# A convolution, attention and expert kernel on one core: the first image, its spectra and the last mixing stores change queues at the seam between two stages

## The chip, the cores and the metric

One core of one Trainium2 chip runs the whole program. The metric is the device time of one execution in microseconds (us), as the median of several runs. Busy times, spans and waits come from one profiled execution, whose own time stands beside them.

## What is computed

The input `x` has 32 images of 128 channels and 64 by 64 pixels, in float32. Two layers follow each other:

```
# layer 0: group norm, a 2-D transform along both axes, a mix of channels at each
#          frequency, the inverse transform, and the image is added
x_f  = tensor_product(gn(x), k11, k12)            # complex, 64 x 64
w_f  = tensor_product(weight, kd1, kd2) * 64
prod = einsum('bihw,oihw->bohw', x_f, w_f)
x    = x + real(tensor_product(prod, k21, k22))
# layer 1, on tokens (pixels) of 128 channels
t = t + attention(ln(t), Wk, bk, Wv, bv)          # for each image a 128 x 128 softmax, made over its tokens
t = t + experts(ln(t), router_w, expert_w)        # 8 experts, the best 2 weighed
```

The kernel arranges the attention of layer 1 image by image: a Gram matrix of the normed tokens, the key and value matrices on either side of it, a softmax of 128 x 128, and one product for all tokens.

## The kernel before

The kernel has three stages, each with a plan of its own (`Plan`): operations get an engine, an estimated duration, a due time, what they follow, and the buffers that they take and free; the plan plays this through and the instructions are recorded in the order that comes out. Before the third plan a list `first` is recorded without any plan.

**Stage 1** (to about 940 us) norms and transforms every image and writes its spectrum to `xf` in DRAM.

**Stage 2, the mixing** (to about 2544 us) runs over the 64 frequencies `w`. For each it builds the weights' spectrum (`weights`, L626), multiplies (`mix`, L648) and copies the result from PSUM to the tiles `outs[half]`: ACT copies rows `hh = 0` and DVE rows `hh = 1` (`mix_out`, L658, tile `o`). `store` (L667) then writes each half of the outputs with eight DMAs of 128 KB on SP's queue to `pf` in DRAM. Half 0 holds output channels 0 to 63, half 1 the others.

**Stage 3** runs over the images. The spectrum of image `b` is read back from `pf` in eight tiles `r` (e = 0 to 7, 16 output channels each; `load_r`, L836, two DMAs of 256 KB for each tile, one for 64 partitions). Tiles 0 to 3 need half 0 of the stores, tiles 4 to 7 half 1. Then come the inverse along w (`w_inverse_piece`, L900, tile `pw`, copied to `u` by ACT, L907), the inverse along h (`h_inverse_piece`, L919, tile `pz`, added to the image `y` by DVE, L927), the turn into tokens (L1001, L1006), the statistics and the norm (L973 to L1041), the Gram matrix (L1052), the key and value products (`kv1`, `kv2`, L1069 and L1077), the softmax, the product with the tokens (L1125), the router and the experts (L1276). Images overlap: the experts of one run beside the front of the next ones.

At the seam between stages 2 and 3 the program holds, in this order:

- `prepare` (L780 to L802), first in `first`: the mean over the model dimension is taken out of the expert weights (two matmuls `pm`, L785; DVE L786 and L790), of the key and value weights `wkv` (matmul `pmk`, L793; DVE L794 and L798), and the router's column sums `rws` are made (matmul `pms`, L801; DVE L802).
- The tiles r 0 and 1 of image 0 on GpSimd's queue, r 2 and 3 on ACT's, then r 4 to 7, r 0 and 1 of image 1, and the images `y0` and `y1` (one DMA of 2 MB each, L830) on SP's.
- The loads of the small constants `wkv`, `rb_sb`, `prx`, `kvb` on ACT's queue (L755 to L778). They, and the eight memsets of `rank` on GpSimd (L763), lie in memory that the tiles `o` held before, so they wait for the last stores of `pf`.

Where the recorded instructions of an engine stand decides what waits behind what: all four engines and SP work through their own lists in order. Of DMA completions there are eight semaphores that SP and ACT use in turn, and eight for GpSimd's queue; a DMA that takes a semaphore again waits until the DMA before it on that semaphore has landed.

Of the kernel before, what the change touches and what calls it, by code (L numbers as in the profile page):

```python
# [10 lines left out]
F32 = mybir.dt.float32  # L11
# [5 lines left out]
P = 128  # L17
# [3 lines left out]
NE = 8  # L21
# [69 lines left out]
def kernel(  # L91
# [15 lines left out]
    nc = tc.nc  # L107
    B = x.shape[0]
    xv = x.rearrange("b c h w -> b c (h w)")
# [3 lines left out]
    n = HW  # L113
# [39 lines left out]
    om = cp.tile([P, P], F32, name="om")  # L153
# [9 lines left out]
    with ExitStack() as ph1:  # L163
# [9 lines left out]
        made, xs, zs, vs, tile_of = {}, {}, {}, {}, {}  # L173
        on_pe = []

        def add(key, engine, us, at, run, after=(), take=(), free=(), late=0.0):
            after = [made[k] for k in after if k in made]
            if engine == "PE":
                after += on_pe[-1:]
            made[key] = plan.add(engine, us, SLOT * at, run, after, take, free, late)  # L180
            if engine == "PE":
                on_pe.append(made[key])
# [248 lines left out]
        def store(b, g):  # L431
            def run():
                f = tile_of.pop(("f", b, g))

                for k in range(0, 8, 4):
                    nc.sync.dma_start(xf[b, :, 8 * g + k : 8 * g + k + 4, :], f[:, k : k + 4])
            return run
# [52 lines left out]
        def piece(kind, b, g, at):  # L490
            if not 0 <= b < B:
                return
            if kind == "pz":
                add(
                    ("pz", b, g), "PE", 1.0, at, turn_over(b, g), [("nm", b, k) for k in range(4)],
                    ("ps",), ("x",) if g == 3 else (),
                )
                for r in range(2):
                    add(
                        ("zo", b, g, r), "ACT", 1.2, at, turned(b, g, r),  # L500
                        [("pz", b, g)] + [("pv", b - 2, k) for k in range(8)] + ([("zo", b, 0, 0)] if g or r else []),
                        (), ("ps",) if r else (),
                    )
            elif kind == "pv":
                add(
                    ("pv", b, g), "PE", 1.12, at, along_w(b, g),
                    [("zo", b, k, r) for k in range(4) for r in range(2)] + ["wi"], ("ps",),
                )
                add(
                    ("vo", b, g), "ACT", 1.02, at, w_out(b, g),  # L510
                    [("pv", b, g)] + [("pf", b - 2, k) for k in range(8)] + ([("vo", b, 0)] if g else []), (), ("ps",),
                )
            else:
                add(("pf", b, g), "PE", 1.95, at, along_h(b, g), [("vo", b, k) for k in range(8)], ("ps",))
                on_act = g % 4 == 3
                add(("fo", b, g), "ACT" if on_act else "DVE", 1.02 if on_act else 1.22, at, h_out(b, g), [("pf", b, g)], ("f",), ("ps",))
                add(("fs", b, g), "SP", 0.9, at, store(b, g), [("fo", b, g)], (), ("f",), 5.0)
# [7 lines left out]
        for s in range(B + 2):  # L525
            if s == 0:
                norm(2)
            for g in range(4):
                at = s + 0.25 * g
# [27 lines left out]
            if 12 <= s < 16:  # L557
                k = s - 12
# [7 lines left out]
    with ExitStack() as ph2:  # L566
# [11 lines left out]
        made, tile_of = {}, {}  # L578
# [84 lines left out]
        def store(w, half):  # L663

            for c in range(0, n, 8):
                lo = (half * n + c) * n
                nc.sync.dma_start(  # L667
                    pf[w, :, lo : lo + 8 * n], outs[half][w % 2 * n : w % 2 * n + n, c : c + 8].rearrange("m o h -> m (o h)")
                )

# [21 lines left out]
        def mixed(*after):  # L692

            while rest:
                w, half, g, at = rest.pop()
                add(
                    ("mo", w, half, g, 1), "DVE", 1.25, at + 0.1, lambda: mix_out(w, half, g, 1),
                    [("mo", w, half, g, 0), *after], (), ("m",),
                )
                if g:  # L700
                    add(
                        ("st", w, half), "SP", 0.1, at + 0.2, lambda: store(w, half),
                        [("mo", w, half, g, hh) for g in range(2) for hh in range(2)], (), ("o",), 8.0,
                    )

        for w in range(n):
# [9 lines left out]
            for half in range(2):  # L716
                for t in range(4):
                    at = w + 0.5 * half + 0.125 * t
# [25 lines left out]
    eps = ctx.enter_context(tc.tile_pool(name="eps", bufs=3, space=PSUM))  # L744
# [23 lines left out]
    QX = P + 2 * NE  # L768
    prx = [ct.tile([P, QX], F32, name=f"prx{i}") for i in range(2)]
    for t in prx:  # L770
        nc.scalar.dma_start(t[:, P + NE : QX], router_w)
    rws = ct.tile([P, NE], F32, name="rws")
# [7 lines left out]
    def prepare():  # L780

        for half in range(2):
            es = slice(4 * half, 4 * half + 4)
            pe = eps.tile([P, 512], F32, tag="pe", name=f"pm{half}")
            nc.tensor.matmul(pe, om, ew_sb[:, es, :].rearrange("d e c -> d (e c)"), start=True, stop=True)  # L785
            nc.vector.scalar_tensor_tensor(  # L786
                ebb[:, es, :].rearrange("p e c -> p (e c)"), ebb[:, es, :].rearrange("p e c -> p (e c)"),
                1.0 / P, pe, ALU.mult, ALU.subtract,
            )
        nc.vector.tensor_add(ew_sb, ew_sb, ebb)  # L790

        pe = eps.tile([P, 512], F32, tag="pe", name="pmk")
        nc.tensor.matmul(pe[:, 0 : 2 * P], om, wkv.rearrange("d e c -> d (e c)"), start=True, stop=True)  # L793
        nc.vector.scalar_tensor_tensor(  # L794
            kvb.rearrange("p e c -> p (e c)"), kvb.rearrange("p e c -> p (e c)"), 1.0 / P, pe[:, 0 : 2 * P],
            ALU.mult, ALU.subtract,
        )
        nc.vector.tensor_add(wkv, wkv, kvb)  # L798

        pe = eps.tile([P, 512], F32, tag="pe", name="pms")  # L800
        nc.tensor.matmul(pe[:, 0:NE], om, prx[0][:, P + NE : QX], start=True, stop=True)  # L801
        nc.vector.tensor_scalar_mul(rws, pe[:, 0:NE], float(P))  # L802

    plan = Plan({"cv": 1, "pe": 3, "tl": 3, "r": 10, "x": 2, "xg": NG, "xn": 2, "xT": 2, "tm": 2, "so": 2, "gate": 2})
    SLOT = 114.0
# [16 lines left out]
            engine, us, SLOT * at, run, [made[k] for k in names if k[0] >= 0], take, free, late  # L822
        )

    xs, rs, tile_of, first = {}, {}, {}, [prepare]

    def transfers(b):
        def load_x():
            xs[b] = xp.tile([P, HW, HW], F32, tag="x", name=f"y{b}")
            nc.sync.dma_start(xs[b].rearrange("c h w -> c (h w)"), xv[b])  # L830

        def load_r(e, queue=nc.sync):
            def run():
                t = rs[b, e] = rp.tile([P, 16 * n], F32, tag="r", name=f"r{b}_{e}")
                for r in range(2):
                    queue.dma_start(t[r * n : (r + 1) * n], pfv[b, e, r])  # L836
            return run

        if b == 0:

            first.extend(load_r(e, nc.gpsimd if e < 2 else nc.scalar) for e in range(4))

        for e in range(8):
            early = b == 0 and e < 4
            add(
                b, f"r{e}", "SP", 0.2, b - 0.5 + 0.08 * e, (lambda: None) if early else load_r(e), take=("r",),
                late=0.0 if early else 5.0,
            )
        add(b, "x", "SP", 0.1, b + 0.2, load_x, take=("x",), late=12.0)

    def conv(b):
        def w_inverse(e):
# [113 lines left out]
    def front(b):  # L966
# [53 lines left out]
        for g in range(8):  # L1020
            at = s1 + 0.016 * g
# [36 lines left out]
        for g in range(8):  # L1058
            at = s1 + 0.26 + 0.016 * g
# [45 lines left out]

        at = s1 + 0.40
        add(b, "gs", "DVE", 0.3, at, gsum, ["pg7"], (), ("tl",))
        add(b, "pb", "PE", 0.35, at, kv1, ["gs"], ("tl",))
        add(b, "t1", "DVE", 0.3, at, kv1_out, ["pb"])
        add(b, "pb2", "PE", 0.35, at, kv2, ["t1"])  # L1110
        add(b, "sm", "DVE", 0.5, at, soft1, ["pb2"])
# [45 lines left out]
        for j, lo in enumerate(range(0, NT, 3)):  # L1157
            m = min(3, NT - lo)
            at = s1 + 0.45 + 0.016 * j
# [71 lines left out]
        at = s1 + 0.64  # L1231
# [130 lines left out]
    for b in range(B):  # L1362
        transfers(b)
        conv(b)
        front(b)
        experts(b)
    with tc.manual_schedule():
        for run in first:
            run()
        plan.run()  # L1370

# [32 lines left out]
def build(arrays):  # L1404
    import concourse.bacc as bacc

    nc = bacc.Bacc("TRN2", target_bir_lowering=False, num_devices=1)
    args = [
        nc.dram_tensor(k, a.shape, mybir.dt.from_np(a.dtype), kind="ExternalInput").ap() for k, a in arrays.items()
    ]  # L1410
    shape = arrays["in_x_dram"].shape
    args.append(nc.dram_tensor("out_0_dram", shape, F32, kind="ExternalOutput").ap())
    with tile.TileContext(nc) as tc:
        kernel(tc, *args)
    return nc
# [8 lines left out]
```

## Time and profile before

| | |
|---|---|
| median of 3 runs | 6112.17 us (6111.25 to 6116.16) |
| the profiled execution's own time | 6110.47 us |
| its span, first to last instruction | 6108.6 us |
| busy: PE, weight loads | 5903.2 us (97%), 4682.8 us (77%) |
| busy: DVE, ACT, POOL | 4245.8 us (70%), 3762.1 us (62%), 4183.5 us (68%) |
| last matmul of stage 2 starts to end | 2535.01 us to 2544.56 us |
| first inverse along w (L900) starts | 2567.96 us |

PE is TensorE's matmuls, PEld its weight loads, DVE VectorE, ACT ScalarE, POOL GpSimd, SP SyncE; a q behind an engine's name is its sequencer, which issues DMAs. L667 is line 667 of the kernel. The chain of waits is the work that ended last, followed back from the end: at each step what released it. "Issue" is time in which an engine waited for nothing that the profile shows. A float32 matmul shows as two records, so a piece of 16 matmuls is 32 records.

### The profile page before, as it was taken

What the parts mean: (1) busy time and instruction counts of PE and PEld (TensorE: products, weight loads), DVE (VectorE), ACT (ScalarE), POOL (GpSimd) and SP (SyncE); (2) the same over time, 40 slices, a digit from 0 to 9 for tenths busy, and PEclk for the clock granted to TensorE, in tenths of its full rate; (3) what the DMA queues carried; (4) which work ended last, traced back from release to release, by engine and by line L of the source; (5) the groups of instructions that cost most, each with busy time, mean ns of one, the idle gap of its engine ahead of it and who ended that gap; (6) DMA issues with size and microseconds to landing.
All of it is one profiled execution on the core that took longest, in us unless ns stands there. A gap on an engine that the chain in (4) does not pass through costs nothing.

```text
span 6108.6 us, 219213 instructions
## 1 busy us (share of the span) xinstructions
PE 5903.2 (97%) x95372; PEld 4682.8 (77%) x95372; DVE 4245.8 (70%) x7696; ACT 3762.1 (62%) x7057; POOL 4183.5 (68%) x3753
## 2 busy tenths in 40 slices
PE   7999999999999999889999999999999999999998
PEld 7999998999999999776666666666666666666654
DVE  5565545555555555458878787787878878787888
ACT  7666664555555555366676676666767676666653
POOL 2110006666666666338888888888888888888888
PEclk9999999999999999899999999999999999999999
DMA  5767666666666666632223132221322223132100
GB/s 200 234 228 237 234 211 182 173 175 172 170 172 173 172 173 173 164 87 92 77 62 103 58 97 70 82 86 60 99 65 90 77 66 100 58 97 70 65 25 28
DMA packets 557732, 756.74 MB, mean 124 GB/s; under 512 B 58592, under 2 KB 322784, under 8 KB 552672
## 3 DMA queue, kind: packets, MB, share of 16 engines
q1 hardware_dynamic: 555120, 740.33, 40.7%
q8 instruction: 749, 12.27, 0.9%
q10 hardware_dynamic: 1328, 1.32, 0.1%
q14 instruction: 215, 1.76, 0.1%
q0 software_dynamic: 320, 1.05, 0.1%
HBM read 406.93 MB, written 335.54 MB: 122 GB/s over the span
## 4 chain that ended last, share of the span: by engine, by line
PE 78%; DVE 9%; ACT 3%; DMA 2%; issue 2%; POOL 0%; SPq 0%; ACTq 0%; POOLq 0%; DVEq 0%
PE pe L1276 24%; PE m L648 17%; PE g L626 9%; PE pf L418 5%; PE pu L857 4%; PE pp L1125 4%; PE py L879 4%; PE pg L1052 4%; DVE tm L1287 2%; PE pv L396 2%; DMA out_dram<-so 2%; PE px L1263 2%; DVE eq L1200 1%; DVE eq L1199 1%; PE po L1322 1%
## 5 line engine op out<-in xcount | busy, mean ns | idle before, releaser
L1276 PE MATMUL pe<-ew_sb,xT 128*128 128x512 f32 x4096 | 1964.9, 601 | 80.1 <-DVE tm L1287 75.1
L1287 DVE TENSOR_TENSOR tm<-pe,oh 128x512 f32<-128x512 f32 x2028 | 1348.6, 685 | 360.8 <-PE pe L1276 339.6
L1312 POOL TENSOR_TENSOR tm<-tm 128x512 f32<-128x512 f32 x1014 | 1281.0, 1278 | 229.4 <-DVE tm L1287 205.7
L1276 PEld LDWEIGHTS pe<-ew_sb,xT 128*128 128x128 f32 x4096 | 701.1, 191 | 591.6 <-issue 405.1
L637 DVE COPY f<-g 128x1024 f32<-128x1024 f32 x512 | 627.2, 1225 | 661.3 <-PE g L626 661.3
L648 PE MATMUL m<-f,s 128*64 128x64 f32 x32768 | 1069.0, 224 | 4.8 <-POOL s L599 3.4
L648 PEld LDWEIGHTS m<-f,s 128*64 128x64 f32 x32768 | 998.4, 138 | 66.6 <-POOL s L599 3.7
L599 POOL COPY s<-l 128x512 f32<-128x512 f32 x512 | 545.4, 1099 | 594.0 <-issue 514.6
L637 ACT COPY f<-g 128x1024 f32<-128x1024 f32 x512 | 519.3, 1014 | 574.6 <-PE g L626 548.0
L1315 POOL TENSOR_TENSOR tk<-tk,tm 128x256 f32<-128x256 f32 x1014 | 758.7, 748 | 79.5
L867 ACT COPY u<-pu 64x512 f32<-64x512 f32 x960 | 557.5, 581 | 223.7 <-PE pu L857 214.3
L1313 POOL TENSOR_TENSOR tm<-tm 128x512 f32<-128x512 f32 x507 | 651.5, 1285 | 39.8
L626 PE MATMUL g<-c,wst 9*128 9x128 f32 x16384 | 607.4, 284 | 4.5 <-ACT f L637 3.3
L626 PEld LDWEIGHTS g<-c,wst 9*128 9x128 f32 x16384 | 508.9, 187 | 40.7 <-ACT f L637 4.4
L857 PEld LDWEIGHTS pu<-qw,r 128*128 128x128 f32 x3840 | 464.4, 193 | 93.3 <-issue 68.7
L1138 ACT ACTIVATE pp<-pp,m 128x128 f32<-128x128 f32 x1024 | 444.3, 434 | 136.7 <-PE pp L1125 110.8
L349 POOL TENSOR_TENSOR grstd<-gms,mhalf 128x1 f32<-128x1 f32 x32 | 17.7, 555 | 737.2 <-DVE gms L345 737.2
L601 POOL TENSOR_SCALAR s<-l 128x512 f32<-128x512 f32 x256 | 509.5, 1990 | 0.0
L418 PE MATMUL pf<-ph,v 128*128 128x128 f32 x4096 | 491.4, 278 | 5.4 <-ACT z L383 1.1
L857 PE MATMUL pu<-qw,r 128*128 128x128 f32 x3840 | 471.7, 276 | 8.0 <-ACT u L867 8.0
L418 PEld LDWEIGHTS pf<-ph,v 128*128 128x128 f32 x4096 | 467.1, 192 | 15.4 <-ACT z L383 7.2
L973 DVE BATCH_NORM_STATS2 bs<-tk 128x6 f32<-128x128 f32 x2048 | 453.1, 280 | 21.9 <-ACT tk L1006 7.0
(164 smaller groups left out, 8228.3 us busy)
## 6 DMA issues: line engine op xcount, KB each, us to landing
xf<-f SPq DMA_DIRECT2D x512, 256.0 KB, 3.3
l<-xf SPq DMA_DIRECT2D x1024, 128.0 KB, 3.1
pf<-o SPq DMA_DIRECT2D x1024, 128.0 KB, 3.2
r<-pf SPq DMA_DIRECT2D x504, 256.0 KB, 4.7
x<-in_x_dram SPq DMA_DIRECT2D x256, 256.0 KB, 4.5
y<-in_x_dram SPq DMA_DIRECT2D x32, 2048.0 KB, 11.3
out_dram<-so SPq DMA_DIRECT2D x256, 256.0 KB, 3.8
tw<-in_tw_dram SPq DMA_DIRECT2D x6, 384.0 KB, 6.5
```

Of the source, the lines that this page charges most:

```text
L418: nc.tensor.matmul(pl[:, j * P : (j + 1) * P], vs[b][:, 8 * g + j, :], ph.rearrange("h r m -> h (r m)"), start=True, stop=True,)
L599: nc.gpsimd.tensor_copy(dst, src)
L626: nc.tensor.matmul(pg[g // 2][:, g % 2, m * P : (m + 1) * P], wst[rows, 16 * half + 4 * t + m, :], c[rows].rearrange("r h k -> r (h k)"), ...
L637: copy(f.rearrange("i m (g o) -> i m g o", g=2), tile_of["g", w, half, t][k].rearrange("i g (o m) -> i m g o", o=4))
L648: nc.tensor.matmul(ps[hh * n : (hh + 1) * n, q, :], s[:, h].rearrange("i k b -> i (k b)")[:, B * r : B * r + n], f[:, h, r, :], start=(r = ...
L857: nc.tensor.matmul(ps[:, k, :], rs[b, e][:, k * P : (k + 1) * P], qw.rearrange("w r m -> w (r m)"), start=True, stop=True,)
L867: nc.scalar.copy(u[r * n : (r + 1) * n, :, oh * n + 8 * e : oh * n + 8 * e + 8], ps[oh * n : (oh + 1) * n, :, r * n : (r + 1) * n].rearran ...
L1276: nc.tensor.matmul(ps, tile_of["xT", b, i // 4][:, i % 4, :], ew_sb[:, es, :].rearrange("d e c -> d (e c)"), start=True, stop=True,)
L1287: nc.vector.tensor_tensor(tile_of["tm", b, i // 2][:, i % 2, es, :], tile_of.pop(("pe", b, i, half)).rearrange("p (e c) -> p e c", c=P), t ...
L1312: nc.gpsimd.tensor_tensor(tm[:, k, 0:4, :], tm[:, k, 0:4, :], tm[:, k, 4:8, :], ALU.add)
L1313: nc.gpsimd.tensor_tensor(tm[:, :, 0:2, :], tm[:, :, 0:2, :], tm[:, :, 2:4, :], ALU.add)
L1315: nc.gpsimd.tensor_tensor(t[:, lo : lo + 2, :], t[:, lo : lo + 2, :], tm[:, :, m, :], ALU.add)
```

## The change

Three things change at the seam, and nothing else:

- Of the very last eight stores of `pf` (w = 63, half 1), those with c = 8, 24, 40, 56 go to ACT's queue.
- Image 0 (`y0`) is loaded first of all, in eight DMAs of 256 KB on GpSimd's queue; behind it on the same queue come the tiles r 0 to 5 of image 0. SP keeps r 6 and 7. ACT's queue has no r tile any more.
- `prepare` keeps the expert weights and is recorded after these loads. The rest becomes two operations of the plan: `kvp` on PE (both matmuls into one PSUM tile) after `h0`, and `kvq` on DVE (its three instructions); `kv1` waits for `kvq`.

```diff
             for c in range(0, n, 8):
                 lo = (half * n + c) * n
-                nc.sync.dma_start(
+                queue = nc.scalar if w == n - 1 and half and c % 16 else nc.sync
+                queue.dma_start(
                     pf[w, :, lo : lo + 8 * n], outs[half][...]
                 )
...
-        pe = eps.tile([P, 512], F32, tag="pe", name="pmk")
+    def prepare_front():
+        pe = tile_of["kvp"] = eps.tile([P, 512], F32, tag="pe", name="pmk")
         nc.tensor.matmul(pe[:, 0 : 2 * P], om, wkv.rearrange("d e c -> d (e c)"), start=True, stop=True)
+        nc.tensor.matmul(pe[:, 2 * P : 2 * P + NE], om, prx[0][:, P + NE : QX], start=True, stop=True)
+
+    def prepared_front():
+        pe = tile_of.pop("kvp")
         nc.vector.scalar_tensor_tensor(kvb..., 1.0 / P, pe[:, 0 : 2 * P], ALU.mult, ALU.subtract)
+        nc.vector.tensor_scalar_mul(rws, pe[:, 2 * P : 2 * P + NE], float(P))
         nc.vector.tensor_add(wkv, wkv, kvb)
...
-    xs, rs, tile_of, first = {}, {}, {}, [prepare]
+    xs, rs, tile_of, first = {}, {}, {}, []
...
-            nc.sync.dma_start(xs[b].rearrange("c h w -> c (h w)"), xv[b])
+            if b == 0:
+                for k in range(8):
+                    nc.gpsimd.dma_start(xs[b][:, 8 * k : 8 * k + 8], x[b][:, 8 * k : 8 * k + 8])
+            else:
+                nc.sync.dma_start(xs[b].rearrange("c h w -> c (h w)"), xv[b])
...
-            first.extend(load_r(e, nc.gpsimd if e < 2 else nc.scalar) for e in range(4))
+            first.append(load_x)
+            first.extend(load_r(e, nc.gpsimd) for e in range(6))
...
-        add(b, "pb", "PE", 0.35, at, kv1, ["gs"], ("tl",))
+        add(b, "pb", "PE", 0.35, at, kv1, ["gs", (0, "kvq")], ("tl",))
...
+            add(0, "kvp", "PE", 0.5, 0.5, prepare_front, ["h0"], ("pe",))
+            add(0, "kvq", "DVE", 1.2, 0.5, prepared_front, ["kvp"], (), ("pe",))
...
-        for run in first:
+        for run in (*first, prepare):
             run()
```

More of the change, by code (lines that the diff above doesn't have):

```diff
@@ L797, in prepare @@
         )
+        nc.vector.tensor_scalar_mul(rws, pe[:, 2 * P : 2 * P + NE], float(P))
         nc.vector.tensor_add(wkv, wkv, kvb)
-        pe = eps.tile([P, 512], F32, tag="pe", name="pms")
-        nc.tensor.matmul(pe[:, 0:NE], om, prx[0][:, P + NE : QX], start=True, stop=True)
-        nc.vector.tensor_scalar_mul(rws, pe[:, 0:NE], float(P))
     plan = Plan({"cv": 1, "pe": 3, "tl": 3, "r": 10, "x": 2, "xg": NG, "xn": 2, "xT": 2, "tm": 2, "so": 2, "gate": 2})
@@ L839, in transfers @@
         if b == 0:
-            first.extend(load_r(e, nc.gpsimd if e < 2 else nc.scalar) for e in range(4))
+            first.append(load_x)
+            first.extend(load_r(e, nc.gpsimd) for e in range(6))
         for e in range(8):
-            early = b == 0 and e < 4
+            early = b == 0 and e < 6
             add(
@@ L848, in transfers @@
             )
-        add(b, "x", "SP", 0.1, b + 0.2, load_x, take=("x",), late=12.0)
+        add(b, "x", "SP", 0.1, b + 0.2, load_x if b else (lambda: None), take=("x",), late=12.0 if b else 0.0)
     def conv(b):
@@ L1364 @@
         conv(b)
+        if b == 0:
+            add(0, "kvp", "PE", 0.5, 0.5, prepare_front, ["h0"], ("pe",))
+            add(0, "kvq", "DVE", 1.2, 0.5, prepared_front, ["kvp"], (), ("pe",))
         front(b)
```

## The prediction

> **What bounds the kernel now.** The page first: PE is busy 97% of the span, so a change off PE's path pays only where PE stands still. The clock row and the chain then show one such place beside the end of stage 1: the seam. The chain of waits from 2535 us on:
>
> ```profile
> 2535.08 2.04 PE m L648 x64
> ...
> 2541.86 1.83 SPq L667
> 2543.73 5.59 DMA pf<-o
> 2549.48 0.50 ACTq L836
> 2550.02 1.01 ACT o L658
> 2551.06 1.24 DVE o L658
> 2552.31 5.21 DMA pf<-o
> 2557.54 0.45 SPq L667
> 2558.03 3.25 DMA pf<-o
> 2561.49 4.71 DMA wkv<-in_wkT_dram
> 2566.22 4.31 DMA r<-pf
> 2571.24 9.13 PE pw L900 x237
> 2580.37 3.08 issue
> 2583.45 9.90 PE pw L900 x242
> 2593.44 0.60 ACT u L907
> ```
>
> Columns: start, length, what. The last copy of `o` waits on ACT behind an r load, the last eight stores behind that copy, the constants behind the stores, and PE behind the constants. Who stood idle is told by the timeline (in brackets the idle time before, and what ended it):
>
> ```profile
> 2550.02 1.00 ACT L658 COPY o<-m 64x1024 f32<-64x1024 f32 x1 [8.14 <-DMA pf<-o]
> ...
> 2551.06 1.23 DVE L658 COPY o<-m 64x1024 f32<-64x1024 f32 x1 [3.85 <-ACT o L658]
> ...
> 2561.55 0.30 POOL L763 MEMSET rank<- 128x1 f32 x8 [15.20 <-DMA pf<-o]
> ```
>
> The last `m` ends at 2544.56, so this copy is 5.4 us late for no reason of data. By stretches (busy us of PE, PEld, DVE, ACT, POOL with counts; granted clock; DMA share; GB/s):
>
> ```profile
> 2569.00:2577.00 8.00, 6.70 (x148) 6.51 (x146) 0.92 (x3) 2.35 (x4) 0.00 (x0) 0.59 1.00 245
> 2579.00:2588.00 9.00, 5.92 (x134) 5.83 (x132) 0.00 (x0) 2.35 (x4) 0.00 (x0) 0.69 1.00 411
> ```
>
> In the first only r tiles move, at 245 GB/s (one DMA of 256 KB lands each 1.05 us) with the DMA engines full. In the second the images move at 411 GB/s. PE runs at a clock of 0.59 to 0.69 there: while it does, a piece of `pw` takes 1.7 us, at full clock 0.93 us (the spacing of the `u` copies).
>
> The target is the end of the inverse along w, 2593.4 us. What follows (h inverse, turns, statistics, w inverse of image 1) is PE and ACT in a chain until the steady state; the recorded order of every engine is unchanged from there to the end, so a shift of 2593.4 reaches the end whole.
>
> **The change, step by step.**
>
> *The copies.* Without r 2 in front, ACT copies at 2544.6 to 2545.6. DVE now has one `ebb` operation before its copy, not two: 2545.66 + 0.69, then 1.23: done at 2547.6 instead of 2552.29, 4.7 us earlier.
>
> *The stores.* SP needed 2552.31 to 2558.63 for eight issues (0.45 to 0.65 us each, and a wait for a landing); four on each queue is about 2.4 us. But their semaphores must have come free from the half 0 stores, the last of which landed at 2550.84 beside 1 MB of r loads; now 2 MB of image are beside them. I take issue to 2551 and, at 3.5 to 5 us from issue to landing, all landed by 2554.5 (2552.5 if the image is out of the way, 2557 if it is not) instead of 2561.28: 6.8 us earlier.
>
> *The image.* `y0` waits for the last `m` (it lies where stage 2's tiles lay), so GpSimd issues it from about 2545.1: eight at 0.5 to 0.8 us. Loads of the same shape ran at 406 GB/s at the start of stage 1 (8 to 20 us), so 2 MB need 5.2 us alone and 8 with the stores. They run in 2546 to 2554, when little else can. In itself this gains nothing: `y0` landed at 2585.89 and DVE first needed it at 2599.60. What it buys is 2 MB less between r and `y1`.
>
> *The r tiles, now the bound.* Before, r 0 to 3 had landed by 2557.2; now GpSimd's list is `y0`, the first DMA of r 0, the memsets of `rank` (which wait for all last stores), then eleven DMAs of 256 KB. Their issue starts at about 2555.2 (0.52 us each, never the bound); the first takes 5.2 us to land, as the quickest of the four on this queue did (up to 6.1): PE starts `pw` at 2560.4 instead of 2567.96, and without the 3.28 us in which it stood for `kvb`. The eleven DMAs are 2.9 MB. Alone at 250 GB/s r 5 would land at 2570. From 2561 SP brings r 6, 7 and image 1's r 0, 1 beside them (seven DMAs after its first one, each held until a constant on ACT has landed), then `y1`. No row shows two queues of r loads side by side: from 245 GB/s together (r rows) to 342 (r and stores, 2556 to 2558). At 310, half for each, GpSimd needs 1.7 us for 256 KB: with 1.5 us to land, r 2 at 2566, r 3 at 2569.5, r 4 at 2573, r 5 at 2576, or 2580 where the 16 KB packets of `y1` come beside its last ones; I take 2578. Bounds for r 5: 2570 and 2584.
>
> *PE.* Tiles 0 to 3 at about 3.4 us each in the slow clock follow the data, tile 4 to 2576.5, tile 5 to 2581, tiles 6 and 7 another 3.7 us (full clock) to 6.8: `pw` ends at 2585, bounds 2580 (data early, clock up at half-way) and 2591, instead of 2593.4: **8.4 us earlier**.
>
> *Key and value preparation.* Its two matmuls (1.19 and 0.43 us) and three DVE operations (0.42, 0.16, 0.42) leave the start and go between the fourth and fifth of the eight `pz` pieces, each 0.69 us of DVE to 0.93 or 1.7 of PE. PE's 32 free records at the slow clock cover part of the DVE time; a `pz` piece three places on waits for the shared PSUM buffers. I charge **1.2 us** (0.6 to 2). `kv1` comes over 40 us later (2652): the added wait costs nothing.
>
> *Instruction gaps.* The "issue" gaps of 3.08 and 3.52 us (2594.64) in PE come while the instruction queue's 16 KB packets arrive among full DMA engines. The engines stay full, so I leave them in; either can go or a third come: 3.5 us each way.
>
> Sum: 8.4 - 1.2 = 7.2 us less than the profiled execution's 6110.47 (span 6108.6 and 1.9 around it): 6103.3. The median stands 1.7 us above that execution, so **6105.0 us**.
>
> **A rule against the change.** The row: at 2556 to 2558 stores on SP's queue and r loads on ACT's moved together at 342 GB/s. The Trainium skill, "DMA: Bandwidth & Descriptors", section "Issuing engines are not separate DMA queues", says that queues of different engines run on the same 16 DMA engines and that spreading saves only the time of issuing. By it the split of the stores would be worth the 3 us of issue, and two r streams would share 245 GB/s: 2.1 us for each of the last eight DMAs instead of 1.7, 3.2 us later, 6108 on the median's scale. The trace's 342 is for another mix, so it does not refute it.
>
> **Rivals.**
>
> *More comes free (0.31).* Two streams, mostly to different halves of the partitions, run near the 342; r 5 lands at 2572 and PE, busy from 2560, gets the full clock by 2574: `pw` ends at 2580 (13.4 earlier), and with `y0` gone one instruction gap goes too (up to 3.5). For it: `y0` and `y1` held the DMA engines full through 2579 to 2593. Against: SP's r 6, 7 and the next image's compete with tiles that are needed first. 13.4 + 1.5 - 1.2 = 13.7: 6098.5.
>
> *Given back (0.20).* r 0 to 5 behind `y0` on one queue arrive so late that the early start is only a longer wait: r 5 at 2583 to 2584, `pw` at 2590 to 2592: 0 to 2 us less, 6110 to 6112. In this case the change doesn't do what it says.
>
> *Slower (0.10).* GpSimd's queue starves beside SP's, which has `y1` in packets of 16 KB against its 4 KB. Break-even: `pw` must end by 2592.2, so r 5 must land by 2586.6 (three tiles at 1.87 us); issue at 2555.2, first data 1.8 us after it (as at 2542.95) and 1.5 us to land: 2.9 MB in 28 us, 103 GB/s. Below that it is slower than before; at 75 GB/s r 5 lands at 2597 and the kernel takes 10 us more, 6122. For it: SP's r DMAs behind the images took 18 us to land. Against: GpSimd's own packets moved at 100 to 270 GB/s beside SP's stores in 2546 to 2550.
>
> **How the numbers follow.** My forecast has 0.39. The range goes from 6096 (the first rival with a whole gap gone) to 6113 (given back, with 2 us of preparation); the slow tail is left out. 0.2%, about what a measurement of this kernel can tell from no change, is 12.2 us: below 6100.0 counts as faster, above 6124.4 as slower. Two thirds of the first rival (0.21) and the low end of my forecast (0.11) lie below: 0.32 faster. Of the slower case only its far end, under 72 GB/s, lies above: 0.06. The rest, 0.62, is within.
>
> **What would show it.** Right: no idle time on ACT before the last copy of `o`; last store landed near 2554.5; `pw` starting near 2560 and ending near 2585, PE waiting in it for r on GpSimd's queue; everything after the turn of image 0 shifted by one constant. Wrong: stores that land after 2558; a `pw` that ends before 2581 or after 2591; a wait of DVE for the eight pieces of `y0`; a shift at 2600 us that is no longer there at 2700.

## Result: the same time, and what the profile after shows

The changed kernel takes 6115.99 us (median of 12 runs, 6110.95 to 6119.93) beside 6114.12 us for the kernel before (12 runs, 6111.25 to 6117.77): ratio 1.0002, 95% interval 0.9994 to 1.001, that is 4 us less to 6 us more. The forecast was 7.2 us less. Single runs of one kernel differ by several us, so the seam is read from the profiles, and all times below that have no word on them are counted **from the start of the last block of mixing matmuls `m`** (2535.01 us in the profile before, 2533.03 after), which takes out what drifted earlier.

The chain of waits of the kernel after, through the seam (start, length, what):

```profile
2533.10 9.48 PE m L648 x320
...
2545.65 0.51 ACTq L668
...
2547.80 9.19 DMA pf<-o
...
2557.30 0.30 POOL rank L764 x8
...
2557.93 5.63 DMA r<-pf
...
2563.85 12.51 DMA r<-pf
...
2576.49 0.69 PE pw L909 x16
2577.18 3.62 issue
2580.79 6.04 PE pw L909 x72
...
2590.89 0.59 ACT u L916
```

The first link did what it should: nothing of ACT's r loads is left in it. The timeline of ACT and GpSimd (in brackets the idle time before and what ended it):

```profile
2542.62 1.00 ACT L658 COPY o<-m 64x1024 f32<-64x1024 f32 x1 [2.73 <-PE m L648]
...
2543.24 4.57 POOL L836 DMA_DIRECT2D y<-in_x_dram  x8 [29.30 <-PE m L648]
2547.80 0.53 POOL L844 DMA_DIRECT2D r<-pf  x1
2557.30 0.30 POOL L764 MEMSET rank<- 128x1 f32 x8 [8.96 <-DMA pf<-o]
2557.93 4.03 POOL L844 DMA_DIRECT2D r<-pf  x8 [0.33 <-issue]
```

The copy of the last `o` starts as soon as the matmul is done; the 8.14 us of idle time before it are gone. But the last of eight stores takes 9.19 us to land beside the image, and GpSimd, which has issued the image and one r DMA, stands 8.96 us at the memset of `rank` until it has. Behind that memset stand eleven r DMAs. By stretches (busy us of PE, PEld, DVE, ACT, POOL with counts; granted clock; DMA share; GB/s), and the queues of 2566 to 2578 us:

```profile
2544.00:2557.00 13.00, 0.49 (x2) 0.00 (x0) 3.50 (x4) 0.00 (x0) 4.34 (x9) 0.65 0.78 266
2577.00:2581.00 4.00, 0.39 (x12) 0.27 (x8) 0.00 (x0) 0.00 (x0) 0.00 (x0) 0.72 1.16 280
2581.00:2585.00 4.00, 4.00 (x79) 4.00 (x78) 0.00 (x0) 1.17 (x2) 0.00 (x0) 0.50 0.93 379
```

```profile
q0 software_dynamic: 477, 1.57, 51.3%
q1 hardware_dynamic: 426, 1.42, 46.4%
```

Columns of the second: packets, MB, share of the 16 DMA engines. GpSimd's queue (q0) moved 1.57 MB in 12 us, SP's (q1) 1.42 MB: 131 and 118 GB/s, hardly more together (249) than one queue of r loads moved alone before (245). The second r DMA of the chain is the last of r 4; PE stood 0.88 us for it. PE then stands 3.62 us for nothing that the profile shows as a wait, and works at a clock of 0.5 after it.

Where the time went, step by step, with the experiments that follow beside it (us from the start of the last `m` block; "last u" is the start of the last of image 0's sixteen `u` copies, the end of `pw` as the prediction counted it; "first tk" is the first copy of image 0's turn):

| kernel | last store landed | pw starts | last u | first y addition | first tk |
|---|---|---|---|---|---|
| before | 26.3 | 33.0 | 58.4 | 64.6 | 74.8 |
| after | 24.0 | 30.6 | 57.9 | 63.1 | 73.8 |
| 1 image behind r (timed profile) | 22.3 | 13.8 | 45.7 | 50.9 | 65.8 |
| 2 rank early | 24.3 | 25.4 | 48.0 | 52.6 | 69.1 |
| 3 preparation alone | 27.7 | 14.6 | 45.4 | 52.6 | 66.9 |
| 4 ACT free alone | 23.0 | 29.3 | 55.1 | 60.6 | 71.9 |
| 5 all but image and r 4, 5 | 23.5 | 14.2 | 43.4 | 48.3 | 63.0 |
| 6 stores alone | 19.2 | 41.1 | 73.7 | 78.3 | 88.4 |
| 7 constants on GpSimd | 23.0 | 14.1 | 59.2 | 69.1 | 77.4 |
| 8 the same, next image behind | 22.4 | 14.3 | 45.7 | 49.8 | 67.0 |
| 9 after, next image behind | 23.3 | 29.9 | 57.8 | 64.0 | 76.1 |
| 10 gates away, image on GpSimd | 24.4 | 15.5 | 44.0 | 49.2 | 62.3 |
| 11 gates away, image on SP | 24.9 | 15.9 | 41.7 | 44.5 | 59.7 |

After gains 2.3 us on the stores and on the start of `pw`, 0.6 on its end and 1.0 at the first tk. Times of single runs that are not named below: experiment 4 took 6109.39 us, with 6115.45 for the kernel before beside it; experiments 7 and 10 took 6126.47 and 6112.95, with 6123.26 beside them; experiments 8 and 9 took 6103.83 and 6108.52, with a median of 6112.81 beside them.

### The profile page after: what moved, and what is told of

It reads as the page before. It is cut to its first block, busy times and chain, and to the rows that moved or that the text cites. A ratio compares the mean times of both kernels' runs of the same rounds, so it can differ in the third digit from the quotient of the medians.

```text
span 6109.2 us, 219231 instructions
## 1 busy us (share of the span) xinstructions
PE 5898.0 (97%) x95372; PEld 4676.7 (77%) x95372; DVE 4247.7 (70%) x7696; ACT 3752.0 (61%) x7057; POOL 4188.0 (69%) x3769
## 4 chain that ended last, share of the span: by engine, by line
PE 78%; DVE 9%; ACT 3%; DMA 2%; issue 2%; POOL 0%; SPq 0%; ACTq 0%; POOLq 0%; DVEq 0%
PE pe L1285 24%; PE m L648 17%; PE g L626 9%; PE pf L418 5%; PE pu L866 4%; PE pp L1134 4%; PE py L888 4%; PE pg L1061 4%; DVE tm L1296 2%; PE pv L396 2%; DMA out_dram<-so 2%; PE px L1272 2%; DVE eq L1209 1%; DVE eq L1208 1%; PE po L1331 1%
## 5 line engine op out<-in xcount | busy, mean ns | idle before, releaser
L648 PEld LDWEIGHTS m<-f,s 128*64 128x64 f32 x32768 | 998.4, 138 | 66.9 <-POOL s L599 4.1
L626 PEld LDWEIGHTS g<-c,wst 9*128 9x128 f32 x16384 | 507.8, 187 | 40.5 <-ACT f L637 4.4
```

The lines of the kernel that those rows point to most:

```text
L626: nc.tensor.matmul(pg[g // 2][:, g % 2, m * P : (m + 1) * P], wst[rows, 16 * half + 4 * t + m, :], c[rows].rearrange("r h k -> r (h k)"), ...
L648: nc.tensor.matmul(ps[hh * n : (hh + 1) * n, q, :], s[:, h].rearrange("i k b -> i (k b)")[:, B * r : B * r + n], f[:, h, r, :], start=(r = ...
```

## The experiments

### 1. Image behind r 0 to 5

```
-            first.append(load_x)
             first.extend(load_r(e, nc.gpsimd) for e in range(6))
+            first.append(load_x)
```

> The changed kernel with one difference: image 0 stands behind r 0 to 5 on GpSimd's queue, not ahead of them. Times are counted from the start of the last block of mixing matmuls, m (before: last store landed at 26.3 us, pw started at 33.0, ended at 58.4; after: 24.0, 30.6, 57.9). Theory 'image': the 2 MB ahead of the last stores are what held them (11.3 us from first issue to last landing, where 9.0 were needed before). Then the last store lands at 19 to 21 us, r 0's second half 6 us later, pw starts at 26 to 27 and, with the same 2 us for each r DMA behind it, ends at 53 to 55; the image lands about 55 and DVE, which needs it at about 60, does not wait. Rival 'stores by themselves': four stores on each of two queues behind the stores of the other half need their 11 us with or without the image; then last store 23 to 24, pw's end 57 to 58.

Both missed. The last store landed at 22.8, between the two; r tiles now moved beside the stores in the image's place (experiment 6 has the stores with neither). But `pw` started at 14.2, not at 26, and its last u copy came at 45.6, 12 us earlier than after. With r first in the list, r 0 to 2 and half of r 3 were issued at 8 to 16 us, as in the kernel before, and the memset of `rank` came only behind them. These tiles need the stores of the other half only. What the change had cost was the early r tiles. The timeline of ACT in the timed profile shows what then limits:

```profile
2551.10 1.27 ACT L916 COPY u<-pw 128x512 f32<-128x512 f32 x2 [6.13 <-DMA pf<-o]
2552.72 0.59 ACT L916 COPY u<-pw 128x512 f32<-128x512 f32 x1 [0.35 <-PE pw L909]
2556.88 0.39 ACTq L756 DMA_DIRECT2D wkv<-in_wkT_dram  x1
...
2562.36 1.56 ACT L916 COPY u<-pw 128x512 f32<-128x512 f32 x3 [9.05 <-DMA rb_sb<-in_router_b_dram]
```

After three copies ACT stands 9.05 us at its constants, whose tiles lie where the last stores still read. The same kernel timed:

> The kernel of the first experiment again (the change with the image behind r 0 to 5), now timed against the kernel before. In one profile its first tk copy stood 8.6 us earlier after the last block of m than before's. Theory 'a constant shift': what follows the seam is unchanged, so the median is 7 to 10 us below before's, ratio 0.9984 to 0.9989. Rival 'given back': the steady state absorbs it, the median is within 4 us of before's.

6104.03 us against 6112.81, ratio 0.9985 (0.9976 to 0.9994): 8.8 us less, as the constant shift had it.

### 2. Rank set at the start of the program

```
+    rank = cp.tile([P, NE], F32, name="rank")      # beside mhalf, at the start, with its eight memsets
...
-    rank = ct.tile([P, NE], F32, name="rank")      # after the last mixing block
```

> The changed kernel with one difference: the eight cells of rank are set at the start of the program, so that r 0's second half and r 1 to 3 on GpSimd's queue no longer stand behind a memset that waits for all last stores. Counted from the start of the last block of m (after: last store 24.0, pw starts 30.6, r 5 landed 47.3, pw ends 57.9). Theory 'gate': the DMA engines stood half idle (154 to 179 GB/s) between the last stores and the first r, and 1.75 MB of r had to wait for a memset; then these land by 28 to 30 us, pw starts at 24 to 26, r 5 lands at 36 to 40 and pw ends at 48 to 52. Rival 'supply': up to the last store the engines were full with the image, so r only changes places with image and stores: last store at 27 to 28 us, r 5 at 44 to 46, pw ends at 55 to 57, 1 to 3 us earlier than after.

Theory "gate" held, but for r 0 to 3, which were there at 33.1 and not by 30: r 5 landed at 38.5 and the last u copy came at 48.0, 9.8 us earlier than after, while the last store was hardly later (24.3). The kernel differs from after only in when, and into which memory, eight memsets of one column each are written. In one run it took 6112.39 us, before 6115.45; the first tk had gained 4.7 us on after.

### 3. Key and value preparation alone

The kernel before with `prepare_front` and `prepared_front` of the change, queued as `kvp` and `kvq` behind `h0`; all queues as before.

> The kernel before with one part of the change alone: key and value preparation behind the inverse of image 0; the queues, the image and the stores stay as before. Counted from the start of the last block of m (before: r 0 to 3 landed by 22.2 us, last store 26.3, pw starts 33.0, r 7 landed at 42.0, pw ends 58.4). Theory 'preparation': PE held pw back for kvb although four r tiles lay ready; then pw starts at 17 to 22 us, makes three pieces (three PSUM buffers), waits until ACT has issued its constants (30.5 us), and makes thirteen more at 0.93 to 1.7 us: end at 47 to 53, most of what the whole change was made for. Rival 'slow pieces': PE at its low clock and with a gap of 3 us needs its 25 us whenever it starts with ACT's copies at 30.5: end at 56 to 58.

Theory "preparation" held, even a little short of the truth: `pw` started at 14.6, its last u copy came at 45.4, the first tk at 66.9, 7.9 us earlier than before (one run: 6106.86 against 6115.45). This part alone is worth what the whole change was forecast to bring. The last store was even 1.4 us later than before, and the gain came all the same.

### 4. ACT free of r loads alone

```
-            first.extend(load_r(e, nc.gpsimd if e < 2 else nc.scalar) for e in range(4))
+            first.extend(load_r(e, nc.gpsimd) for e in range(4))
```

> The kernel before with r 2 and r 3 of image 0 issued by GpSimd's queue, not by ACT's, and nothing else. Counted from the start of the last block of m (before: ACT's copy of the last o at 15.0 us, last store 26.3, pw starts 33.0, ends 58.4). Theory 'copy': the copy of the last o waited on ACT behind r loads; without them it starts at 9.5 to 10 us, the last store lands at 21 to 22, the constants and r 4 to 7 come 4 to 5 us earlier, pw starts at 28 to 29 and ends at 53 to 54. Rival 'nothing arrives': the stores still wait for landings of earlier stores beside 2 MB of r, so the last one lands at 24 or later, and pw ends at 56 to 58.

Between the two: last store 23.0, last u 55.1, first tk 71.9, 2.9 us earlier than before. The stores moved by 3.2 us of the 5.4 us that the copy gained.

### 5. Everything but the image and r 4, r 5

Experiments 3 and 4 together, and `queue = nc.scalar if w == n - 1 and half and c % 16 else nc.sync` for the last stores.

> The kernel before with three parts of the change and without the fourth: key and value preparation behind the inverse, ACT free of r loads (r 0 to 3 on GpSimd's queue), the last stores by two queues; the image and r 4, r 5 stay on SP's queue. Counted from the start of the last block of m (first turn copy tk: before 74.8, after 73.8; preparation alone 66.9; ACT free alone 71.9). Theory 'sum': last store at 22 to 23, ACT free of its constants at 27 to 28 instead of 32.3, r 7 landed at 38 to 41, pw ends at 42 to 44 and the first tk copy stands at 62 to 64, 7.9 and 2.9 us less than before. Rival 'the image now': pw's end no longer counts, as DVE waits for the image on SP behind r (landed at 47.6 to 52.5 in the two single runs): first y addition at 50 to 53, first tk at 65 to 67.

The "sum" held: first tk at 63.0, 11.8 us earlier than before, and 10.8 earlier than after. Its last store landed at 23.5, with eight stores on SP's queue alone (experiment 4) at 23.0: the second queue shortened the issue (12.6 to 16.0 us instead of 12.7 to 17.3) and not the landing. One run each gave 6105.44 and 6123.26; by the seam it is 12 of these 18 us; single runs cannot tell where the rest lies.

### 6. The stores with nothing of GpSimd's beside them

```
+            first.append(set_rank)      # the eight memsets of rank, which wait for all last stores
             first.append(load_x)
```

> The changed kernel with one difference: GpSimd sets rank (which waits for all last stores) ahead of the image, so that the image and r 0 to 5 all come behind the last stores and nothing of GpSimd's queue moves beside them. Counted from the start of the last block of m (after: stores issued 12.6 to 14.8, last landing 24.0, first r of the gate 30.5, pw starts 30.6, ends 57.9). Theory 'shared engines': the 11 us of the stores were the image's doing (and with the image behind r, that of the r tiles, 22.8). Then the last store lands at 18 to 20, the image by 26 to 27, r 0 at 28 to 30, r 5 at 48 to 51, and pw ends at 58 to 62: about as after, because the image now stands between stores and r. Rival 'their own time': the last store still lands at 22 to 24, r 0 at 32 to 34, r 5 at 53 to 56, and pw ends at 63 to 66.

For the stores "shared engines" held: the last one landed at 19.2 instead of 24.0, so the image, with the one r DMA behind it, had cost them 4.7 us. Its chain of waits has the last store with 4.28 us to land, where after had 9.19:

```profile
2555.78 4.28 DMA pf<-o
...
2560.37 0.31 POOL rank L849 x8
...
2561.11 4.80 DMA y<-in_x_dram
```

The rest went far beyond both expectations: image at 36.7 (26 to 27 expected), r 5 at 65.6, last u at 73.7. Behind the stores everything came at once: between 2568 and 2585 us GpSimd's queue moved 2.12 MB and SP's 2.09 MB, and some 1.3 MB of SP's was for the next image. Once the next image's own packets came (16 KB each, against 4 KB for r tiles), GpSimd's queue fell to 0.28 MB in 5 us, 56 GB/s; the queues from 2585 to 2590 us (packets, MB, share):

```profile
q1 hardware_dynamic: 85, 1.29, 80.3%
q0 software_dynamic: 84, 0.28, 19.0%
```

One run: 6134.61 against 6123.26. This is what the "slower" rival of the prediction described, with the image between stores and r.

### 7 and 8. Constants on GpSimd's queue; then the next image behind them

Experiment 1 with `nc.gpsimd.dma_start` in place of `nc.scalar.dma_start` for wkv, rb, router and kvb.

> The changed kernel with the image behind r 0 to 5 (as in the first experiment) and with the constants (wkv, rb, router, kvb) issued by GpSimd's queue instead of ACT's. Counted from the start of the last block of m (first experiment: pw starts at 14.2, u copies stop from 18 to 29.4, r 5 lands at 33.9, r 7 at 43.6, pw ends at 46.2, first tk at 66.2). Theory 'ACT held': the copies of u stood behind seven constants on ACT, which wait for the last stores; with ACT free r 0 to 2 are worked off by 26, the second half of r 3 comes behind the constants at 31 to 33, r 5 at 36 to 38, r 6 and 7 on SP at 27 to 34, pw ends at 40 to 42 and first tk stands at 60 to 62. Rival 'data': r 3's second half to r 7 and the image set the end as before: pw ends at 45 to 47, first tk at 65 to 67.

Both wrong, and in the other direction: last u at 59.2, first tk at 77.4, later than in the kernel before. ACT was free (copies at 16.9 to 24.3 without a stop), but r 3's second half landed at 39.6 and r 5 at 51.3. The queues from 2570 to 2588 us (28 to 46 from the start of the block):

```profile
q1 hardware_dynamic: 590, 3.57, 75.6%
q0 software_dynamic: 462, 1.09, 26.1%
```

SP's queue had 198 GB/s and GpSimd's 61. In experiment 1 SP's r loads had waited, one by one, for the landings of constants on ACT (19.1 us in all); with the constants elsewhere SP had nothing to wait for and ran ahead to the next image. That waiting had been a brake which nobody had planned. Test of this reading: the next image's r tiles and the next image put on GpSimd's queue, behind image 0's.

```
-                load_r(e)                                    nc.sync.dma_start(xs[b]...)
+                load_r(e, nc.gpsimd if b == 1 else nc.sync)  (nc.gpsimd if b == 1 else nc.sync).dma_start(xs[b]...)
```

> The experiment with the constants on GpSimd's queue (first tk at 77.4, slower than before's 74.8), with one difference: the next image's r tiles and the next image itself stand on GpSimd's queue, behind everything of image 0, not on SP's beside it. Theory 'shared engines': there SP, no longer held by the constants' landings, moved r 1 tiles and the next image (26 to 60 us) beside GpSimd's r 3 to 5, which took 2.2 us per DMA and landed at 39.6 to 51.3. Without them r 5 lands at 35 to 38, pw ends at 41 to 44, the image lands by 44 to 47 and first tk stands at 60 to 64. Rival 'GpSimd's queue by itself': its r DMAs behind the constants keep 2 us or more each, r 5 lands at 46 to 51, pw ends at 55 to 60, first tk at 73 to 77.

r 5 landed at 38.1 and the last u copy came at 45.7, 13.5 us earlier than in experiment 7: the next image's loads were what starved r. The size was missed: first tk at 67.0, not 60 to 64, because r 3's second half still came behind seven constants (32.9), and PE stood 7.4 us for it.

### 9. The changed kernel with the next image behind

> The changed kernel with one difference: the next image's r tiles and the next image itself stand on GpSimd's queue behind r 5, so that only r 6 and r 7 move on SP's queue beside r 0 to 5. Counted from the start of the last block of m (after: r 5 lands at 47.3, 2.0 us per DMA, r 7 at 42.3, pw ends at 57.9, first tk at 73.8). Theory 'shared engines': about 250 GB/s for both queues together, so the 1 MB less beside them brings r 5 in 4 us earlier, at 42 to 44, and pw's end to 53 to 55, first tk to 69 to 71. Rival 'each queue has its own pace': GpSimd's DMAs keep 2 us each, r 5 at 46 to 48, pw's end 57 to 58.

r 5 landed at 45.1, between the two expectations and 2.3 us earlier than after. The pace shows the sharing: beside SP's r 6 and 7 GpSimd's last r DMAs up to 43.0 landed 2.1 to 2.9 us apart; SP's last one landed at 43.3, and the next three of GpSimd's came at 44.0, 45.1 and 46.0. But the last u copy did not move, 57.8 to after's 57.9. The chain says why:

```profile
2565.22 6.01 PE pw L909 x145
2571.23 3.07 issue
2574.30 5.50 PE pw L909 x127
2579.80 3.08 issue
2582.88 5.18 PE pw L909 x87
2588.06 1.51 issue
2589.57 3.51 PE pw L909 x113
```

Nothing of it is a wait for a tile: PE works, stands for two gaps of 3.1 us and one of 1.5, and after each of the long ones the clock is low again (0.67 in the 3 us after the first, 0.54 in 2583 to 2586). Data that come earlier find PE not ready for them.

### 10 and 11. A version made of the parts

From experiment 5, with `rank` at the start and the constants in a pool allocated ahead of the r tiles, so that they lie where nothing of the last stores lay; GpSimd loads them ahead of r 0 to 3. No instruction of ACT or GpSimd then waits for the last stores. First with the image on GpSimd's queue behind r 0 to 3:

```
+    cc = ctx.enter_context(tc.tile_pool(name="cc", bufs=1))    # wkv, rb_sb, prx, kvb and their loads
     rp = ctx.enter_context(tc.tile_pool(name="rp", bufs=10))
```

> A version made of the parts: preparation behind the inverse, last stores by two queues, rank set at the start of the program, the constants in tiles that lie where nothing of the last stores lay (loaded by GpSimd ahead of r), r 0 to 3 and behind them the image on GpSimd's queue, r 4 to 7 on SP's. No instruction of ACT or GpSimd waits for the last stores any more. Counted from the start of the last block of m (after: pw starts 30.6, ends 57.9, first tk 73.8). Theory 'gates': pw starts at 14 to 17, r 0 to 3 land by 24 and are worked off by 27, the last store lands at 23 to 25 and r 7 at 34 to 36, pw ends at 36 to 39, and first tk stands at 53 to 57, 17 to 21 us earlier than after. Rival 'PE itself': at a clock of 0.5 to 0.7 and with one or two gaps of 3 us pw needs its 27 us from the moment the tiles come: end at 44 to 46, first tk at 61 to 65.

The gates opened as expected (constants landed by 8.5, `pw` from 15.5), but the size is the rival's: last u at 44.0, first tk at 62.3. The rival's reason does not hold, though: inside `pw` PE stood 3.8, 0.9 and 2.1 us for r tiles, and no other stop was longer than 0.4 us. The image moved beside r 4 to 7, which landed at 27.6 to 40.5, about 2 us apart. Then with the image back on SP's queue behind them:

> The version of the previous experiment with the image back on SP's queue, behind r 4 to 7 and the next image's first two r tiles (one DMA, as in the kernel before); preparation behind the inverse, two queues for the last stores, rank and constants out of the way of the last stores and r 0 to 3 on GpSimd's queue stay. Counted from the start of the last block of m (previous version: r 4 to 7 landed 27.6 to 41.5 beside the image, pw ended at 44.6, first tk at 62.3; before 74.8; after 73.8). Theory 'shared engines': without the image beside them r 4 to 7 come at 1.05 us per DMA, r 7 at 32 to 35, pw ends at 36 to 39; the image lands at 42 to 46 and is now what DVE waits for: first tk at 57 to 60, and the kernel takes 13 to 18 us less than before. Rival 'PE itself': pw needs until 43 to 45 whatever the data do (low clock, gaps): first tk at 61 to 64, 10 to 13 us less than before.

6099.80 us (11 runs, 6097.56 to 6103.12) against 6112.81: ratio 0.9979 (0.997 to 0.9988), 13.0 us less, the fastest kernel of this case. r 7 landed at 34.2, the image at 44.4 and the first y addition started at 44.5, directly behind it; first tk at 59.7. `pw`'s end missed the theory's 36 to 39: its last u copy came at 41.7. Its chain:

```profile
2549.04 10.30 DMA pf<-o
...
2561.13 6.56 DMA r<-pf
...
2567.82 0.65 PE pw L906 x15
2568.47 4.00 issue
2572.46 5.06 PE pw L906 x113
...
2577.55 0.59 ACT u L913
```

One gap of 4.00 us stood between tiles that lay ready and the end of `pw`. So "shared engines" set the data and "PE itself" the last 4 us.

## Why the prediction was wrong, step by step

**What bounds the kernel, and the copies: right.** ACT's idle time before the last copy of `o` is gone, as said; DVE copies at 11.4, 4.7 us earlier, which was the figure.

**The stores: this step failed.** Taken: landed by 2554.5, that is 19.5 from the start of the block. Measured: 24.0, 4.5 us later and beyond the text's own late bound (2557, or 22.0); the prediction had named landings after 2558 as a sign of being wrong (24.0 is 2559.0 on its axis). Experiment 6 shows the cause: without the image and the r DMA behind it 19.2, almost exactly the value taken. The prediction put the image into "2546 to 2554, when little else can run", at 8 us beside the stores. It took 13 us (10.2 to 23.2), and the stores 4.7 us more.

**The start of `pw`: carried along, and a cost put at nothing.** Taken 25.4, measured 30.6: 4.5 us from the stores, the rest from the memsets of `rank` and a first r landing of 5.63 us. The memset was noted as a wait and costed at nothing beyond the stores' landing. Experiment 2 shows that as a gate it cost 9.8 us at the end of `pw`, because r 0 to 3, which in the kernel before had landed by 22.2, did not need those stores at all.

**The r tiles: rate mis-sized.** Taken 310 GB/s for two streams and 1.7 us per DMA; measured 249 and 2.0. The row chosen for it, 342 GB/s, was of stores beside r loads. The Trainium skill, "DMA: Bandwidth & Descriptors", section "Issuing engines are not separate DMA queues", says that DMAs started by different engines run on the same 16 DMA engines and that a second issuing engine saves only issue time. The trace agrees with that rule here, 249 GB/s for two streams beside 245 for one, and so do the stores of experiments 4 and 5. The split was near the half for each that the sum took between two queues of r tiles (131 to 118 GB/s), but 61 to 198 where SP's also had the next image (experiment 7).

**PE: a term that was too small.** From start to last u copy 24.6 us were taken, 27.2 measured. Where neither ACT's constants nor late tiles hold `pw` for long once it has started, this time is 25.5 (before), 25.9 (experiment 4), 25.8 (experiment 11), 27.2 (after) and 27.9 (experiment 9); in experiment 10 it is 28.5, of which 6.7 are waits for tiles. Each of the five has at least one gap of 3.1 to 4.0 us in it, and after it two or three pieces at up to 1.7 us instead of 0.93. It is not a fixed time of PE: in experiment 2 the gaps were 2.4, 1.2 and 1.2 us, no slow pieces followed them, and `pw` took 22.6 us. The sum counted the gaps as unchanged and took the pace from the data's arrival; in after PE stood still for 6.9 us inside `pw`, and only 0.9 of them were for a tile. Thus of the 7.9 us by which the end of `pw` was missed (50.0 taken, 57.9 measured), 5.2 are its start and 2.6 its pace; r 5, which the text called the bound, was not it (experiment 9).

**Preparation: cost right, gain overlooked.** The fourth and fifth y additions start 2.15 us apart in after (2600.35 and 2602.50) where the pieces next to them stand 0.93 apart: 1.2 us, as charged. But taking it out of PE's way is worth 7.9 us by itself while r 0 to 3 still come early (experiment 3). The change takes that away in the same step, as its image goes ahead of them.

**The rivals.** "Given back" is the one that happened by its numbers: r 0 to 5 behind the image on one queue, 0 to 2 us less, `pw`'s end 0.6 us earlier. Its r 5 at 2583 to 2584 lies close to the measured 47.3 (2582.3 on that axis). Its reason is not what was seen: it had an early start of `pw` eaten up by a late r 5, but `pw` started only 2.3 us earlier, and r 5 was not what held its end. It had 6110 to 6112; the median lies higher, 3 us above the range, as the scatter of runs and the kernel before's own median (6114.12 with 12 runs, 6112.17 with three) allow. The seam itself gives no reason for more than before. "More comes free" fell with the 249 GB/s. "Slower" did not occur in after, but its mechanism is real: experiment 7 had GpSimd's queue at 61 GB/s, below its break-even of 103, and a first tk 2.5 us later than before.

**Open.** The gaps without a wait have a mark that the profiles show, though no run tried it. Between the first `pw` and the first tk there are 49 of them over 0.45 us in the fourteen profiles, and in every one PE goes on 1.3 to 1.7 us after a 16 KB packet of the instruction queue has landed; in after the packets landed at 37.6, 46.2, 53.0 and 60.7, and PE went on at 39.1, 47.8, 54.3 and 62.2. Inside `pw` of after and of experiments 2 and 9 they also stand at the same places of PE's list, after 145, 272 and 399 of the 512 records. So PE seems to stand there for its next instructions; the prediction had noted these packets and left the gaps in unchanged. Why those come late is open: the DMA engines are full at the time in each kernel, but no run took that load away. Also open is where the rest of a gain stays behind the seam: experiment 11 is 16.8 us ahead of before at the last u copy, 15.1 at the first tk and 13.0 in the medians.

## What to carry to other kernels

Before a load is moved to the front of a queue, list what stood there and what it was waiting for: here four tiles that needed only older stores went behind 2 MB that nobody needed until 40 us after they had landed, and behind memsets of one column that waited for the last store. A tile's place in memory is a gate too; constants and small memsets belong where nothing late has lain. And a wait that looks useless can be a brake on another queue: count what it lets loose before taking it away.

## What the hardware showed that was not expected

- Two queues with loads waiting on both were served about packet for packet, not byte for byte. With 4 KB packets on both, r tiles beside r tiles moved at 131 and 118 GB/s (477 and 426 packets). Beside the next image's 16 KB packets on SP's queue, GpSimd's queue moved as many packets and a quarter of the bytes or less: 84 to 85 packets, 56 against 258 GB/s in the 5 us shown in experiment 6. No run changed the packet size alone.
- A gap can cost PE more than its length. After the 3.62 us gap of the kernel after, the granted clock was 0.50 for the next 4 us and two u copies came in that time; in 2585 to 2589 it was 0.93. In experiment 2, after gaps of 2.4, 1.2 and 1.2 us, it stayed at 1.00 (2569 to 2599 us). The Trainium skill, "TensorE: Matmul & The Clock Gate", section "Part 1: The HAM clock gate (the "warmup" mystery)", states half the clock after an idle window of about 3.4 us and the full clock after as long a busy one. The stretches here agree in the two levels, 0.50 from 2578.7 to 2585.5 us and 1.00 on both sides of it in after, but not in the start: the clock fell 1.5 us after the gap had begun, and in experiment 10 it fell within a gap of 2.6 us (1.00 until 2587.9 us, 0.50 from 2588.0).
- Eight stores of 128 KB needed 9.19 us from the last issue to the last landing beside 2 MB of image, and 4.28 us without it.
